# A triangle update followed by a gated pair layer: how the turn from rows to channels is ordered

## The chip, the cores and the metric

The kernel runs on one core of one Trainium2 chip. A core has a matrix engine (PE, with its weight loads shown apart as PEld), a vector engine (DVE), an activation engine (ACT), a general engine (POOL) and a synchronisation engine (SP) that here only issues DMA transfers. Each engine runs its own queue of instructions in order and waits for the others through semaphores. The metric is the device time of one execution in microseconds; lower is better. Three runs of the kernel before took 3364.26, 3364.52 and 3364.75 us; the median is 3364.52 us.

## The reference, cut to what matters

The input x is a square of 384 x 384 positions with 128 channels, all float32. Two layers follow each other.

```python
# layer 0
z_n = layernorm(z)                                   # over the 128 channels
a = (z_n @ Wa + ba) * sigmoid(z_n @ Wga + bga)
b = (z_n @ Wb + bb) * sigmoid(z_n @ Wgb + bgb)
x = einsum('bijd,bjkd->bikd', a, b)                  # for each channel d: a 384x384 matrix product
x = layernorm(x)                                     # over the channels
y = z + (x @ Wo + bo) * sigmoid(z_n @ Wgo + bgo)
# layer 1, on pair = y
left  = pair @ W_left + b_left + pair @ W_eq + b_eq
right = sum over k of (pair @ W_right + b_right)     # one vector for each row i
out   = (left * right * sigmoid(pair @ W_gate + b_gate)) @ W_out + b_out
return layernorm(out + pair)
```

The norm over channels in the middle and the product over j are at odds: a and b are made position by position with all channels, and the product wants one channel with all positions. So a and b are turned from one layout to the other by way of the chip's main memory.

## The kernel before, in words

The kernel has three phases, each written out as a fixed order of instructions; nothing is reordered by a scheduler. Waits between engines and the reuse of tile buffers are derived from the program by the tile layer: an instruction waits for the last users of the memory that it overwrites and for the writers of what it reads, in on-chip memory and in main memory alike.

**Phase 1, by rows.** The square is cut into NT = 72 tiles of 128 rows by CX = 16 columns; tile n covers row block n // 24 and columns 16 (n mod 24) onwards. A tile is worked in TS = 4 steps of CT = 4 columns, so there are 288 steps. For each step s the function `step` (line 199) puts the work in this order. PE: projections pga, pa, pgb (`proj`, line 215), the transposes of the next step's normalised input (`turn`, line 168), pb, and the output gate's projection pgo (line 252). ACT: the sigmoid of pga, the sigmoid of the step before's output gate into the tile gt (`gate`, line 178), two normalisations of a later step, the sigmoid of pgb, the copy of the turned input from PSUM to the tile zT (`turned_out`, line 171), two more normalisations. DVE: statistics of a later tile, the gated at (line 234), the gated bt (line 247), and pgo plus its bias into gs (line 254). The results leave for four arrays in main memory: A[d, j, i] and B[d, j, k] by channel, G (the output gates) and Z (x plus the last bias) by position. POOL issues A (line 238), G (line 185) and Z (line 160), each 1 MB for a tile. B is gathered over CG = 64 columns, four tiles, in a tile bt of 32 KB in each partition; SP issues it in four pieces of BR = 32 rows and 1 MB (`store_b`, line 266), one piece at the end of each following tile, so that the pieces of a group leave during the next group. The last group has no next group: after the last step all pieces that remain go out at once (line 264). Rows of B in such a piece are 64 columns, 256 bytes, long.

On-chip buffers of phase 1 that matter here: four xt tiles, two of each at, gt, bt and zb, three zT, three gs, six PSUM banks for projections (pk) and two for the transposes.

**Phase 2, by channels.** For each channel d, `fetch` (line 433) loads A[d] and B[d] whole, 0.59 MB each, through SP; `product` (line 447) does three products of 128 rows by 384, each of NB = 3 matmuls that add up over the three thirds q of j. Channel 0 is kept as x0 (ACT, line 456). For the others DVE subtracts x0 (line 459), ACT squares (line 464), POOL and DVE keep the running sums s1 and s2 (lines 466 and 445), and SP stores the result to X (line 467). LAST = 8 channels of loads fit on chip; loads run AHEAD = 6 channels in front, and the last eight channels are done block of rows by block of rows so that `deviation` (line 394), the norm's factors, can start early.

**Phase 3, by rows again.** It reads X, G and Z (`load`, line 379), applies the norm and layer 0's output, and does layer 1. The change leaves its instructions as they are; some of its tiles lie elsewhere.

SP's queue thus carries, in order: the loads of xt with the B pieces between them, then the loads of A and B by channel with the stores of X between them, then phase 3's loads. An SP transfer also waits for the one eight places before it.

Of the kernel before, what the change touches and what calls it, by code (L numbers as in the profile page):

```python
# [19 lines left out]
def kernel(ctx: ExitStack, tc: tile.TileContext, ins, out: bass.AP):  # L20
# [25 lines left out]
    A = dram.tile([P, N, N], FP, tag="A", name="A")  # L46
# [31 lines left out]
    wT, bcol = {}, {}  # L78
# [3 lines left out]
    def over(t, n):  # L82
        return t[:, None, :].to_broadcast([P, n, C])
# [4 lines left out]

    CG, CX, CT, BR = 64, 16, 4, 32
    TS = CX // CT
    NT = NB * (N // CX)
    with tc.tile_pool(name="wprep", bufs=6) as wp, tc.tile_pool(name="p1x", bufs=4) as px, tc.tile_pool(name="p1s", bufs=3) as ps, tc.tile_pool(
        name="p1o", bufs=2
    ) as po, tc.tile_pool(name="p1t", bufs=2, space=PSUM) as ppt, tc.tile_pool(
        name="p1p", bufs=6, space=PSUM
    ) as ppp:
        tiles, turned, bts, gated, b_out_of = {}, {}, {}, {}, []
# [5 lines left out]
        def fetch(n):  # L105
            for _ in fetch_parts(n, 1):
                pass
# [46 lines left out]
        def residual(n):  # L154
            if n >= NT:
                return
            r0, c0 = place(n)
            zb = po.tile([P, CX, C], FP, tag="zb", name=f"zb_{n}")
            nc.gpsimd.tensor_tensor(zb, tiles[n]["x"], over(b_out, CX), ALU.add)  # L159
            nc.gpsimd.dma_start(out=Z[r0 : r0 + P, c0 : c0 + CX, :], in_=zb)  # L160

# [9 lines left out]
        def turned_out(s):  # L171
            if s // TS >= NT:
                return
            zT = ps.tile([P, CT, P], FP, tag="zT", name=f"zT_{s}")
            nc.scalar.copy(zT, turned[s])  # L175
            turned[s] = zT

        def gate(s):
            n, t = divmod(s, TS)
            gs = gated.pop(s)  # L180
            gt = tiles[n]["gt"]
            nc.scalar.activation(gt[:, t * CT : (t + 1) * CT, :], gs, AF.Sigmoid)
            if t == TS - 1:
                r0, c0 = place(n)
                nc.gpsimd.dma_start(out=G[r0 : r0 + P, c0 : c0 + CX, :], in_=gt)
                tiles.pop(n - 1, None)


        CATCH_UP = 3 * TS
# [9 lines left out]
        def step(s):  # L199
            n, t = divmod(s, TS)  # L200
            r0, c0 = place(n)
            if t == 0:
                fetch(n + 3)
                if s >= CATCH_UP:
                    norm_factors(n + 1)
                tiles[n]["at"] = po.tile([P, CX, P], FP, tag="at", name=f"at_{n}")
                tiles[n]["gt"] = po.tile([P, CX, C], FP, tag="gt", name=f"gt_{n}")
                if c0 % CG == 0:
                    bts[n // (CG // CX)] = po.tile([P, P, CG], FP, tag="bt", name=f"bt_{n}")
            at, bt = tiles[n]["at"], bts[n // (CG // CX)]  # L210
            k0 = c0 % CG + t * CT
            zT = turned.pop(s)
            ahead = (n + 1, t - 1) if t else (n, TS - 1)

            def proj(k):
                pk = ppp.tile([P, CT, P], FP, tag="pk", name=f"p{k}_{s}")
                nc.tensor.matmul(pk, lhsT=wT[k], rhs=zT, start=True, stop=True)  # L217
                return pk

            def sigmoid(k, pg):  # L220
                sg = ps.tile([P, CT, P], FP, tag="sg", name=f"sg{k}_{s}")
                nc.scalar.activation(sg, pg, AF.Sigmoid, bias=bcol["g" + k])  # L222
                return sg

            statistics(columns_ahead(s), columns_ahead(s + 1))
            for factors in FIRST_FACTORS.get(s, ()):
                norm_factors(*factors)
            pga, pa = proj("ga"), proj("a")
            sga = sigmoid("a", pga)
            if s:  # L230
                gate(s - 1)
            if s >= CATCH_UP:
                normalise(*ahead, range(CT // 2))
            nc.vector.scalar_tensor_tensor(  # L234
                at[:, t * CT : (t + 1) * CT, :], pa, bcol["a"], sga, ALU.add, ALU.mult
            )
            if t == TS - 1:
                nc.gpsimd.dma_start(out=A[:, c0 : c0 + CX, r0 : r0 + P], in_=at)  # L238
            pgb = proj("gb")
            sgb = sigmoid("b", pgb)  # L240
            turn(s + 1)
            turned_out(s + 1)
            if s == 0:
                normalise(0, 2)
            normalise(*ahead, range(CT // 2 if s >= CATCH_UP else 0, CT))
            pb = proj("b")
            nc.vector.scalar_tensor_tensor(  # L247
                bt[:, :, k0 : k0 + CT].rearrange("d r c -> d c r"), pb, bcol["b"], sgb, ALU.add, ALU.mult
            )
            pgo = ppp.tile([P, CT, C], FP, tag="pk", name=f"pgo_{s}")  # L250
            for c in range(CT):
                nc.tensor.matmul(pgo[:, c, :], lhsT=zT[:, c, :], rhs=wT["go"], start=True, stop=True)  # L252
            gs = ps.tile([P, CT, C], FP, tag="gs", name=f"gs_{s}")
            nc.vector.tensor_tensor(gs, pgo, over(gate_bias, CT), ALU.add)
            gated[s] = gs
            if s < CATCH_UP:
                if s in FIRST_RESIDUALS:
                    residual(FIRST_RESIDUALS[s])
            elif t == 1:
                residual(n + 1)  # L260
            if k0 + CT == CG:
                b_out_of.extend((bt, r0, c0 + CX - CG, k) for k in range(0, P, BR))
            if t == TS - 1:
                store_b(len(b_out_of) if n == NT - 1 else 1)

        def store_b(pieces):
            for bt, r0, k0, r in b_out_of[:pieces]:
                nc.sync.dma_start(out=B[:, r0 + r : r0 + r + BR, k0 : k0 + CG], in_=bt[:, r : r + BR, :])
            del b_out_of[:pieces]

        def weight(k, q):
            w = wp.tile([P, P], FP, tag="w", name="w_" + k)
# [85 lines left out]
        for s in range(NT * TS):  # L358
            step(s)
            if s >= CATCH_UP:  # L360
                next(later, None)
        gate(NT * TS - 1)

# [2 lines left out]

    sums = ctx.enter_context(tc.tile_pool(name="sums", bufs=1, reuse_waits="tile"))
    x0, s1, s2, rs0 = (sums.tile([P, NB, N], FP, tag=k, name=k) for k in ("x0", "s1", "s2", "rs0"))
    nc.gpsimd.memset(s1, 0.0)
    nc.gpsimd.memset(s2, 0.0)
    LAST, AHEAD, R = 8, 6, 4
    pl = ctx.enter_context(tc.tile_pool(name="p3l", bufs=3, reuse_waits="tile"))
    group = {}

    def load(u):
# [14 lines left out]
    def deviation(ib, bank):  # L394

        def work(k):
            return sums.tile([P, N], FP, tag="w" + k, name=f"{k}_{ib}")
# [25 lines left out]
        for _ in range(n):  # L423
            next(g, None)

    with tc.tile_pool(name="p2", bufs=LAST, reuse_waits="tile") as p2, tc.tile_pool(
        name="p2s", bufs=12, reuse_waits="tile"
    ) as p2s, tc.tile_pool(name="p2p", bufs=5, space=PSUM, reuse_waits="tile") as pp2, tc.tile_pool(
        name="p2q", bufs=2, space=PSUM, reuse_waits="tile"
    ) as pq2, tc.tile_pool(name="p2t", bufs=1, space=PSUM, reuse_waits="tile") as pt2:  # L430
        factors, squares = {}, []

        def fetch(d):
            if d >= C:
                return
            ad = p2.tile([P, NB, N], FP, tag="ad", name=f"ad_{d}")
            bd = p2.tile([P, NB, N], FP, tag="bd", name=f"bd_{d}")
            nc.sync.dma_start(out=ad, in_=A[d].rearrange("(q p) i -> p q i", p=P))
            nc.sync.dma_start(out=bd, in_=B[d].rearrange("(q p) k -> p q k", p=P))
            factors[d] = ad, bd  # L440
# [6 lines left out]
        def product(d, ib):  # L447
            ad, bd = factors[d]
            pm = pp2.tile([P, N], FP, tag="pm", name=f"pm_{d}_{ib}")
            for q in range(NB):  # L450
                nc.tensor.matmul(  # L451
                    pm, lhsT=ad[:, q, ib * P : (ib + 1) * P], rhs=bd[:, q, :],
                    start=(q == 0), stop=(q == NB - 1),
                )
            if d == 0:
                nc.scalar.copy(by_third(x0[:, ib, :]), pm.rearrange("i (p q) -> i q p", q=NB))
                return
# [8 lines left out]
            nc.gpsimd.tensor_tensor(s1[:, ib, :], s1[:, ib, :], xd, ALU.add)  # L466
            nc.sync.dma_start(out=X[ib][d], in_=xd)

        for d in range(AHEAD):
            fetch(d)  # L470
        for d in range(C - LAST):
            fetch(d + AHEAD)
            for ib in range(NB):
                product(d, ib)
        for d in range(C - LAST + AHEAD, C):
            fetch(d)
        behind = None
        for ib in range(NB):
            if ib == NB - 1:
# [189 lines left out]
```

## Time and profile before

| what | value |
|---|---|
| median of three runs | 3364.52 us |
| the profiled execution's own time | 3363.57 us |
| its span | 3361.8 us |
| PE busy | 3288.6 us, 98% of the span |
| PEld busy | 2191.5 us, 65% |
| DVE busy | 2665.4 us, 79% |
| ACT busy | 2310.0 us, 69% |
| POOL busy | 2093.2 us, 62% |
| DMA | 910.52 MB, mean 271 GB/s |
| phase 1 | from the start to about 1392 us |
| phase 2 | first product at 1423.13 us, last at about 2170 us |

The profile comes from one execution; its span differs from the median of the runs by less than 0.1%. PE's busy time is an average over three phases with different limits, so a wait is read in its own stage. Matmuls are pipelined, and their ends are modelled. In the groups, the columns are the line of the program, engine, operation, what is written and read, the count, then busy time and mean of one in ns, and last the idle time just before, with what ended it. In the chain of waits each line is a start, a length and what the time was spent on. In the tables by stage the pairs are busy time and count of PE, PEld, DVE, ACT and POOL, followed by the clock that PE was granted, the mean busy share of the DMA engines and GB/s.

### The profile page before, as it was taken

What the parts mean: (1) busy time and instruction counts of PE and PEld (TensorE: products, weight loads), DVE (VectorE), ACT (ScalarE), POOL (GpSimd) and SP (SyncE); (2) the same over time, 40 slices, a digit from 0 to 9 for tenths busy, and PEclk for the clock granted to TensorE, in tenths of its full rate; (3) what the DMA queues carried; (4) which work ended last, traced back from release to release, by engine and by line L of the source; (5) the groups of instructions that cost most, each with busy time, mean ns of one, the idle gap of its engine ahead of it and who ended that gap; (6) DMA issues with size and microseconds to landing.
All of it is one profiled execution on the core that took longest, in us unless ns stands there. A gap on an engine that the chain in (4) does not pass through costs nothing.

```text
span 3361.8 us, 53349 instructions
## 1 busy us (share of the span) xinstructions
PE 3288.6 (98%) x15581; PEld 2191.5 (65%) x15581; DVE 2665.4 (79%) x8599; ACT 2310.0 (69%) x5488; POOL 2093.2 (62%) x1574
## 2 busy tenths in 40 slices
PE   8999999999999999699999999999999999999997
PEld 5555555555555555355555555578888888888885
DVE  8877777777777777345555555799999999999998
ACT  7787777877877877422222222378888888888887
POOL 7555555555555555145555555458888888888887
PEclk9999999999999999799999999999999999999998
DMA  6888888888888898799999999767777777777774
GB/s 225 263 262 274 280 277 288 274 284 280 273 263 266 275 282 277 221 340 304 307 304 305 307 306 305 260 228 263 263 264 263 264 263 264 263 263 263 263 264 141
DMA packets 675330, 910.52 MB, mean 271 GB/s; under 512 B 319328, under 2 KB 616288, under 8 KB 647520
## 3 DMA queue, kind: packets, MB, share of 16 engines
q1 hardware_dynamic: 634000, 680.28, 63.0%
q0 software_dynamic: 40320, 226.51, 19.2%
q8 instruction: 126, 2.06, 0.2%
q14 instruction: 164, 1.34, 0.1%
q10 hardware_dynamic: 720, 0.33, 0.0%
HBM read 454.04 MB, written 452.98 MB: 270 GB/s over the span
## 4 chain that ended last, share of the span: by engine, by line
PE 92%; DVE 5%; DMA 1%; POOL 1%; SPq 0%; ACT 0%; issue 0%; POOLq 0%; ACTq 0%; DVEq 0%
PE pm L451 22%; PE pgo L252 8%; PE pga L217 7%; PE pa L217 7%; PE pb L217 7%; PE pgb L217 7%; PE py L546 7%; PE pf L536 7%; PE pleft L587 7%; PE pg L589 6%; PE ptr L168 4%; PE ptr L510 3%; DVE py L552 1%; DVE st L557 1%; DVE h L524 1%; DVE res L537 1%
## 5 line engine op out<-in xcount | busy, mean ns | idle before, releaser
L451 PE MATMUL pm<-bd,ad 128*128 128x384 f32 x2304 | 745.8, 487 | 31.6 <-DMA bd<-B 31.6
L451 PEld LDWEIGHTS pm<-bd,ad 128*128 128x128 f32 x2304 | 438.8, 191 | 337.7 <-issue 33.9
L466 POOL TENSOR_TENSOR s<-s,xd 128x384 f32<-128x384 f32 x381 | 380.2, 998 | 395.6 <-DVE xd L459 395.4
L464 ACT ACTIVATE sq<-xd 128x384 f32<-128x384 f32 x381 | 188.5, 495 | 544.9 <-DVE xd L459 544.9
L247 DVE SCALAR_TENSOR_TENSOR bt<-pb,c_L_conv_bb,sgb 128x512 f32<-128x512 f32 x288 | 321.6, 1117 | 242.6 <-ACT zT L175 232.8
L459 DVE TENSOR_TENSOR xd<-pm,x 128x384 f32<-128x384 f32 x381 | 212.2, 557 | 376.3 <-POOL s L466 321.0
L149 ACT ACTIVATE zn<-xt,off,rstd 128x128 f32<-128x128 f32 x1152 | 503.3, 489 | 2.9 <-POOL off L140 2.8
L579 ACT ACTIVATE res<-res,off,rs 128x128 f32<-128x128 f32 x1152 | 482.3, 485 | 20.4 <-POOL off L573 18.6
L552 DVE SCALAR_TENSOR_TENSOR py<-py,rs,gr 128x128 f32<-128x128 f32 x1152 | 436.6, 379 | 1.6 <-PE py L546 1.0
L238 POOL DMA_DIRECT2D A<-at x72 | 85.5, 1188 | 544.1 <-DVE at L234 544.1
L252 PEld LDWEIGHTS pgo<-wT_go,zT 128*128 128x128 f32 x2304 | 302.5, 192 | 137.7 <-issue 72.0
L222 ACT ACTIVATE sga<-pga,c_L_conv_bga 128x512 f32<-128x512 f32 x288 | 197.9, 687 | 274.8 <-PE pga L217 274.8
L557 DVE BATCH_NORM_STATS2 st<-res 128x6 f32<-128x128 f32 x1152 | 364.4, 317 | 0.3
L619 POOL TENSOR_TENSOR res<-res,r_L_conv_ln_bias 128x1536 f32<-128x1536 f32 x94 | 324.8, 3455 | 7.4
L159 POOL TENSOR_TENSOR zb<-xt,r_L_conv_b_out 128x2048 f32<-128x2048 f32 x72 | 327.1, 4544 | 1.8
L536 PE MATMUL pf<-w_o,h 128*128 128x128 f32 x2304 | 321.2, 276 | 6.1 <-ACT w_o L518 5.3
L618 POOL TENSOR_TENSOR res<-res,r_L_conv_ln_scale 128x1536 f32<-128x1536 f32 x94 | 325.5, 3463 | 0.1
L546 PE MATMUL py<-w_o,xr 128*128 128x128 f32 x2304 | 320.8, 275 | 0.9 <-DVE xd L459 0.9
L594 ACT ACTIVATE sg<-pg,c_L_conv_b_gate 128x384 f32<-128x384 f32 x384 | 223.2, 581 | 141.9 <-PE pg L589 90.5
L587 PE MATMUL pleft<-pairT,m_L_conv_W_left 128*128 128x384 f32 x768 | 313.0, 489 | 2.9 <-ACT pairT L512 2.8
L589 PE MATMUL pg<-pairT,m_L_conv_W_gate 128*128 128x384 f32 x768 | 311.1, 487 | 0.0
L130 DVE BATCH_NORM_STATS2 st<-xt 128x6 f32<-128x128 f32 x1152 | 306.1, 266 | 3.6 <-DMA xt<-in_x_dram 3.6
(131 smaller groups left out, 6818.9 us busy)
## 6 DMA issues: line engine op xcount, KB each, us to landing
A<-at POOLq DMA_DIRECT2D x72, 1024.0 KB, 8.3
Z<-zb POOLq DMA_DIRECT2D x72, 1024.0 KB, 8.2
G<-gt POOLq DMA_DIRECT2D x72, 1024.0 KB, 8.7
B<-bt SPq DMA_DIRECT2D x72, 1024.0 KB, 16.9
ad<-A SPq DMA_DIRECT2D x128, 576.0 KB, 7.0
bd<-B SPq DMA_DIRECT2D x128, 576.0 KB, 8.0
xr<-X SPq DMA_DIRECT2D x96, 768.0 KB, 6.0
gr<-G SPq DMA_DIRECT2D x96, 768.0 KB, 7.6
```

Of the source, the lines that this page charges most:

```text
L149: nc.scalar.activation(g["zn"][:, c, :], g["x"][:, c, :], AF.Identity, bias=g["off"][:, c : c + 1], scale=g["rstd"][:, c : c + 1],)
L217: nc.tensor.matmul(pk, lhsT=wT[k], rhs=zT, start=True, stop=True)
L252: nc.tensor.matmul(pgo[:, c, :], lhsT=zT[:, c, :], rhs=wT["go"], start=True, stop=True)
L451: nc.tensor.matmul(pm, lhsT=ad[:, q, ib * P : (ib + 1) * P], rhs=bd[:, q, :], start=(q == 0), stop=(q == NB - 1),)
L466: nc.gpsimd.tensor_tensor(s1[:, ib, :], s1[:, ib, :], xd, ALU.add)
L536: nc.tensor.matmul(pf[:, q, :], lhsT=h[:, q * P : (q + 1) * P], rhs=w_o, start=True, stop=True)
L546: nc.tensor.matmul(py[:, q, :], lhsT=g["x"][:, i, q * P : (q + 1) * P], rhs=w_o0, start=True, stop=True)
L552: nc.vector.scalar_tensor_tensor(py[:, q, :], py[:, q, :], rs0[:, q, u : u + 1], g["g"][:, i, q, :], ALU.mult, ALU.mult)
L557: nc.vector.bn_stats(b["st"][:, k, q, :], b["res"][:, k, q, :])
L579: nc.scalar.activation(g["res"][:, i, q, :], g["res"][:, i, q, :], AF.Identity, bias=g["off"][:, i, q : q + 1], scale=g["rs"][:, i, q : q ...
L587: nc.tensor.matmul(pleft, lhsT=w_left, rhs=pairT, start=True, stop=True)
L589: nc.tensor.matmul(pg[:, 0:N], lhsT=w_gate, rhs=pairT, start=True, stop=True)
```

## The change

- **Gate projections of the last group.** For the last TG = 4 tiles, steps S2 = 272 to 287, pgo and gs are taken out of `step` into a function `gate_project` and done after all steps, one behind the other, with the sigmoids following one place later. Since zT is then read long after its step, `turned_out` writes it into the tile xt for those steps.
- **The last group's b.** It is not stored by rows. Its tile is allocated so that it stays on chip through most of phase 2 (`pb_held`), and `store_held` stores it by HELD = 16 channels: 16 partitions, 128 rows of 256 bytes, 0.52 MB. The first goes between the loads of the first four channels, the second after those of channel 5, six more inside the loop over channels, at d = 14, 30, 46, 62, 78 and 94.
- **First products by thirds.** Channels 0 to 3 are loaded in two parts: thirds 0 and 1 of j first, which the last row block does not touch, and third 2 after the first held store. The first two thirds of five products (EARLY) are multiplied before the loop, and `product` adds the last third.
- **Memory.** zb uses the memory that later holds x0, s1, s2 and rs0 (`acc`). The two bt tiles come from two pools of one. A[d] and B[d] share one tile ab, and phase 2's tiles are allocated from the other end of on-chip memory. The pools of `deviation` and of phase 3's loads open after the held tile is freed.

The diff without empty lines and without the renamed pools of unchanged tiles:

```diff
+    S2 = (NT - TG) * TS
+    acc = acc.tile([P, 4, NB, N], FP, tag="acc", name="acc")
+    pb_held = held.enter_context(tc.tile_pool(name="p1bh", bufs=1))
...
-            zb = po.tile([P, CX, C], FP, tag="zb", name=f"zb_{n}")
+            zb = acc.rearrange("p a q n -> p (a q n)")[:, (n % 2) * CX * C : (n % 2 + 1) * CX * C]
...
-            zT = ps.tile([P, CT, P], FP, tag="zT", name=f"zT_{s}")
+            if s < S2:
+                zT = ps.tile([P, CT, P], FP, tag="zT", name=f"zT_{s}")
+            else:
+                n, t = divmod(s, TS)
+                zT = tiles[n]["x"][:, t * CT : (t + 1) * CT, :]
...
+        def gate_project(s):
+            n, t = divmod(s, TS)
+            if t == 0:
+                tiles[n]["gt"] = pgt.tile([P, CX, C], FP, tag="gt", name=f"gt_{n}")
+            zT = turned[s]
+            pgo = ppp.tile([P, CT, C], FP, tag="pk", name=f"pgo_{s}")
+            for c in range(CT):
+                nc.tensor.matmul(pgo[:, c, :], lhsT=zT[:, c, :], rhs=wT["go"], start=True, stop=True)
+            gs = ps.tile([P, CT, C], FP, tag="gs", name=f"gs_{s}")
+            nc.vector.tensor_tensor(gs, pgo, over(gate_bias, CT), ALU.add)
+            gated[s] = gs
...
-            if s:
+            if 0 < s <= S2:
                 gate(s - 1)
...
+            if s < S2:
+                gate_project(s)
...
-            if k0 + CT == CG:
+            if k0 + CT == CG and n < NT - 1:
                 b_out_of.extend((bt, r0, c0 + CX - CG, k) for k in range(0, P, BR))
...
+        for s in range(S2, NT * TS):
+            gate_project(s)
+            if s > S2:
+                gate(s - 1)
         gate(NT * TS - 1)
+        b_held = bts[NT // TG - 1]
...
+        def store_held(d):
+            if d < C:
+                nc.sync.dma_start(out=B[d : d + HELD, N - P :, N - CG :], in_=b_held[d : d + HELD])
...
-        for d in range(AHEAD):
+        EARLY = ((0, 0), (0, 1), (0, 2), (1, 0), (1, 1))
+        for d in range(4):
+            fetch(d, 0, NB - 1)
+        store_held(0)
+        for d in range(4):
+            fetch(d, NB - 1)
+        for d in range(4, AHEAD):
             fetch(d)
+        store_held(HELD)
+        for d, ib in EARLY:
+            multiply(d, ib, range(NB - 1))
         for d in range(C - LAST):
             fetch(d + AHEAD)
+            if (d + 2) % HELD == 0:
+                store_held(d + 2 + HELD)
             for ib in range(NB):
                 product(d, ib)
...
+        held.close()
+        work_of = ctx.enter_context(tc.tile_pool(name="work", bufs=1, reuse_waits="tile"))
```

More of the change, by code (lines that the diff above doesn't have):

```diff
@@ L91 @@
     CG, CX, CT, BR = 64, 16, 4, 32
-    TS = CX // CT
+    TS, TG = CX // CT, CG // CX
     NT = NB * (N // CX)
-    with tc.tile_pool(name="wprep", bufs=6) as wp, tc.tile_pool(name="p1x", bufs=4) as px, tc.tile_pool(name="p1s", bufs=3) as ps, tc.tile_pool(
-        name="p1o", bufs=2
-    ) as po, tc.tile_pool(name="p1t", bufs=2, space=PSUM) as ppt, tc.tile_pool(
+    S2 = (NT - TG) * TS
+    acc = ctx.enter_context(tc.tile_pool(name="acc", bufs=1, reuse_waits="tile"))
+    acc = acc.tile([P, 4, NB, N], FP, tag="acc", name="acc")
+    held = ExitStack()
+    pb_held = held.enter_context(tc.tile_pool(name="p1bh", bufs=1))
+    with tc.tile_pool(name="wprep", bufs=6) as wp, tc.tile_pool(name="p1s", bufs=3) as ps, tc.tile_pool(
+        name="p1g", bufs=2
+    ) as pgt, tc.tile_pool(name="p1x", bufs=4) as px, tc.tile_pool(name="p1a", bufs=2) as pa_, tc.tile_pool(
+        name="p1b", bufs=1, side="right"
+    ) as pb_, tc.tile_pool(name="p1t", bufs=2, space=PSUM) as ppt, tc.tile_pool(
         name="p1p", bufs=6, space=PSUM
@@ L157, in residual @@
             r0, c0 = place(n)
-            zb = po.tile([P, CX, C], FP, tag="zb", name=f"zb_{n}")
+            zb = acc.rearrange("p a q n -> p (a q n)")[:, (n % 2) * CX * C : (n % 2 + 1) * CX * C]
+            zb = zb.rearrange("p (x c) -> p x c", x=CX)
             nc.gpsimd.tensor_tensor(zb, tiles[n]["x"], over(b_out, CX), ALU.add)
@@ L205, in step @@
                     norm_factors(n + 1)
-                tiles[n]["at"] = po.tile([P, CX, P], FP, tag="at", name=f"at_{n}")
-                tiles[n]["gt"] = po.tile([P, CX, C], FP, tag="gt", name=f"gt_{n}")
+                tiles[n]["at"] = pa_.tile([P, CX, P], FP, tag="at", name=f"at_{n}")
                 if c0 % CG == 0:
-                    bts[n // (CG // CX)] = po.tile([P, P, CG], FP, tag="bt", name=f"bt_{n}")
-            at, bt = tiles[n]["at"], bts[n // (CG // CX)]
+                    bts[n // TG] = (pb_ if (NT - 1 - n) // TG % 2 else pb_held).tile(
+                        [P, P, CG], FP, tag="bt", name=f"bt_{n}"
+                    )
+            at, bt = tiles[n]["at"], bts[n // TG]
             k0 = c0 % CG + t * CT
-            zT = turned.pop(s)
+            zT = turned[s]
             ahead = (n + 1, t - 1) if t else (n, TS - 1)
@@ L249, in step @@
             )
[L250 to L255, printed above, removed]
+            if s < S2:
+                gate_project(s)
             if s < CATCH_UP:
@@ L260, in step @@
                 residual(n + 1)
-            if k0 + CT == CG:
+            if k0 + CT == CG and n < NT - 1:
                 b_out_of.extend((bt, r0, c0 + CX - CG, k) for k in range(0, P, BR))
[L263 to L267, printed above, removed]
+            if t == TS - 1 and b_out_of:
+                bt, r0, k0, r = b_out_of.pop(0)
                 nc.sync.dma_start(out=B[:, r0 + r : r0 + r + BR, k0 : k0 + CG], in_=bt[:, r : r + BR, :])
-            del b_out_of[:pieces]
         def weight(k, q):
@@ L361 @@
                 next(later, None)
+        for s in range(S2, NT * TS):
+            gate_project(s)
+            if s > S2:
+                gate(s - 1)
         gate(NT * TS - 1)
+        b_held = bts[NT // TG - 1]
     def by_third(t):
         return t.rearrange("i (q p) -> i q p", q=NB)
-    sums = ctx.enter_context(tc.tile_pool(name="sums", bufs=1, reuse_waits="tile"))
-    x0, s1, s2, rs0 = (sums.tile([P, NB, N], FP, tag=k, name=k) for k in ("x0", "s1", "s2", "rs0"))
+    x0, s1, s2, rs0 = (acc[:, k] for k in range(4))
     nc.gpsimd.memset(s1, 0.0)
     nc.gpsimd.memset(s2, 0.0)
-    LAST, AHEAD, R = 8, 6, 4
-    pl = ctx.enter_context(tc.tile_pool(name="p3l", bufs=3, reuse_waits="tile"))
+    LAST, AHEAD, R, HELD = 8, 6, 4, 16
     group = {}
@@ L396, in work @@
         def work(k):
-            return sums.tile([P, N], FP, tag="w" + k, name=f"{k}_{ib}")
+            return work_of.tile([P, N], FP, tag="w" + k, name=f"{k}_{ib}")
         v, t, r, sg, sd = (work(k) for k in ("v", "t", "r", "sg", "sd"))
@@ L424, in advance @@
             next(g, None)
-    with tc.tile_pool(name="p2", bufs=LAST, reuse_waits="tile") as p2, tc.tile_pool(
-        name="p2s", bufs=12, reuse_waits="tile"
+    with tc.tile_pool(name="p2", bufs=1, side="right", reuse_waits="tile") as p2, tc.tile_pool(
+        name="p2s", bufs=12, side="right", reuse_waits="tile"
     ) as p2s, tc.tile_pool(name="p2p", bufs=5, space=PSUM, reuse_waits="tile") as pp2, tc.tile_pool(
@@ L430, with pair_of, fetch @@
     ) as pq2, tc.tile_pool(name="p2t", bufs=1, space=PSUM, reuse_waits="tile") as pt2:
-        factors, squares = {}, []
-        def fetch(d):
+        factors, products, squares = {}, {}, []
+        def pair_of(d):
+            return p2.tile([P, 2, NB, N], FP, tag=f"ab{d % LAST}", name=f"ab_{d}")
+        for d in reversed(range(LAST)):
+            factors[d] = pair_of(d)
+        def fetch(d, q0=0, q1=NB):
             if d >= C:
                 return
[L436 to L440, printed above, removed]
+            if d not in factors:
+                factors[d] = pair_of(d)
+            for k, of in enumerate((A, B)):
+                nc.sync.dma_start(
+                    out=factors[d][:, k, q0:q1], in_=of[d, q0 * P : q1 * P].rearrange("(q p) i -> p q i", p=P)
+                )
+        def store_held(d):
+            if d < C:
+                nc.sync.dma_start(out=B[d : d + HELD, N - P :, N - CG :], in_=b_held[d : d + HELD])
         def add_squares():
@@ L445, in add_squares, with multiply, product @@
                 nc.vector.tensor_tensor(s2[:, ib, :], sq, s2[:, ib, :], ALU.add)
[L447 to L450, printed above, removed]
+        def multiply(d, ib, qs):
+            ab = factors[d]
+            if 0 in qs:
+                products[d, ib] = pp2.tile([P, N], FP, tag="pm", name=f"pm_{d}_{ib}")
+            for q in qs:
                 nc.tensor.matmul(
-                    pm, lhsT=ad[:, q, ib * P : (ib + 1) * P], rhs=bd[:, q, :],
+                    products[d, ib], lhsT=ab[:, 0, q, ib * P : (ib + 1) * P], rhs=ab[:, 1, q, :],
                     start=(q == 0), stop=(q == NB - 1),
                 )
+        def product(d, ib):
+            multiply(d, ib, range(NB) if (d, ib) not in products else range(NB - 1, NB))
+            pm = products.pop((d, ib))
             if d == 0:
@@ L476 @@
             fetch(d)
+        held.close()
+        work_of = ctx.enter_context(tc.tile_pool(name="work", bufs=1, reuse_waits="tile"))
+        pl = ctx.enter_context(tc.tile_pool(name="p3l", bufs=3, reuse_waits="tile"))
         behind = None
```

## The prediction

> **What bounds the kernel now.** I read the table of slices first: PE is at eight or nine tenths nearly everywhere, with one dip to 6 in slice 17, near 1400 us. Then the costliest groups (busy us, mean ns | idle before and its releaser):
>
> ```profile
> L451 PE MATMUL pm<-bd,ad 128*128 128x384 f32 x2304 | 745.8, 487 | 31.6 <-DMA bd<-B 31.6
> ```
>
> All 2304 product matmuls together wait once, 31.6 us, for a load of B. The chain of waits around that place (start us, us, what):
>
> ```profile
> 1390.78 1.10 DVE bt L247
> 1392.30 7.31 SPq L268
> 1399.66 7.50 SPq L268
> 1407.20 11.36 DMA B<-bt
> 1418.65 4.35 DMA bd<-B
> 1423.13 77.08 PE pm L451 x231
> ```
>
> The last b is written at 1391.9; its four 1 MB stores leave until 1418.65, and only then is B loaded. The stages there (busy us of PE, PEld, DVE, ACT, POOL; then granted clock, DMA share, GB/s):
>
> ```profile
> 1380.00:1390.00 10.00, 10.00 (x42) 5.85 (x41) 5.03 (x7) 4.83 (x9) 0.00 (x0) 1.00 0.00 2
> ...
> 1405.00:1410.00 5.00, 0.00 (x0) 0.00 (x0) 0.00 (x0) 0.00 (x0) 0.00 (x0) 0.50 0.85 216
> ...
> 1423.00:1427.00 4.00, 3.87 (x6) 2.19 (x7) 0.00 (x0) 0.00 (x0) 0.00 (x0) 0.50 1.03 362
> ```
>
> DMA does nothing in the 10 us before the turn; then 256-byte pieces move at 216 GB/s while PE stands; then PE restarts at half clock. So this turn is bound by data, everything around it by PE. Last, the timeline of the step before the last one, for what a step is bound by:
>
> ```profile
> 1382.31 1.02 PE L217 MATMUL pga<-zT,wT_ga 128*128 128x512 f32 x2
> ...
> 1384.02 1.02 PE L217 MATMUL pgb<-zT,wT_gb 128*128 128x512 f32 x2
> ...
> 1384.88 0.60 PE L168 MATMUL ptr<-ident,zn 128*128 128x128 f32 x4
> ...
> 1385.14 0.69 ACT L222 ACTIVATE sgb<-pgb,c_L_conv_bgb 128x512 f32<-128x512 f32 x1 [0.57 <-PE pgb L217]
> ...
> 1385.73 0.58 ACT L175 COPY zT<-ptr 128x512 f32<-128x512 f32 x1
> ...
> 1386.18 1.05 PE L252 MATMUL pgo<-wT_go,zT 128*128 128x128 f32 x8
> ...
> 1387.07 1.02 PE L217 MATMUL pga<-zT,wT_ga 128*128 128x512 f32 x2
> ```
>
> Step to step is 4.765 us, filled by PE; pgo holds 0.89 of it. The copy of the next zT ends at 1386.31, while PE is still in pgo.
>
> [...] clock 0.50 until about 1427.7. [...] No store of 16 partitions is in this trace. [...]
>
> **The change part by part.** S is the end of the last step's pb on PE.
>
> 1. *Gate projections of the last 16 steps move behind all steps.* Each step loses 0.89 of PE work: 4.765 − 0.886 = 3.88. But PE was the cover for ACT. The order there is sgb, then the zT copy, and the next pga needs zT. From pga, the copy ends at 1386.31 − 1382.31 = 4.00; a PE matmul started 0.06 after its ACT releaser elsewhere (2178.94 to 2179.00). So a step takes 4.06. ACT's two pairs of zn and DVE's statistics, at and bt (1.8 + 0.75 + 1.1 = 3.65) fit in that. Fifteen intervals by 0.705 = 10.6 us: the last pga falls from 1387.07 to 1376.5. The last step is then pga, pa, pgb, pb, 4 × 0.86 = 3.44: S = 1379.9. Its bt ends at S + 1.4 = 1381.3. The sixteen projections take 16 × 0.886 = 14.2: PE busy until 1394.1. They need nothing that is late: zT now stays in the x tiles. PE's idle inside the steps is 16 × 0.18 = 2.9 us, a real cost.
>
> 2. *What is queued behind the gates.* The gt tile has two buffers. Tile 70's first sigmoid waits until tile 68's G store has landed, and DVE's gs has three buffers, so DVE stalls behind ACT, and the second and third early products wait for the last two gs (PSUM banks). With gs 0.67 and gt 0.62: G of tile 68 is issued at S + 5.5, of tile 69 at S + 9.1. If a G store lands after L us, the last but one gs ends at about S + 8.9 + L, and the second early product could start at S + 15.5. So PE waits about L − 6.3. G landed after 8.4 us at the busy end of phase 1, and 7.8 in a lighter stretch. I take L = 8, a stall of 1.75 us; L = 6 gives 0, L = 12 gives 5.7.
>
> 3. *Loads by thirds, first two thirds early.* In the built program the first load waits for the last store of the group before (issued at 1337.5, 10 us of issue; landed by about 1355) and A of tiles up to 63. Four pairs of two thirds, 3.1 MB, move in the idle stretch; at 216 GB/s they need 15 us: there by 1370, 24 us before use. The five early products are 10 matmuls by 0.643 = 6.4 us of PE work, so the last thirds are wanted at 1394.1 + 1.75 + 6.4 = 1402.3.
>
> 4. *The held b.* SP issues the first 0.52 MB store at 1381.3. The bytes take 2.4 us at 216 GB/s[...]; the first bd load, 0.59 MB, landed in 4.35 us of which 1.6 are bytes at 376 GB/s, so 2.8 us are fixed. That makes 5 to 8 us: landed by 1389. A of tile 71 (issued 1379.5, 6.3 to 8 us) lands by 1387.5. Behind them: the loads of d = 0's last thirds, 4.4 (the first bd load) to 8 us (median): 1393 to 1397. Slack 5 us or more; cost nothing, with the projections and early products as cover. The later loads have more time: d = 4 is wanted at about 1419. Traffic until then: A 1.05, G 4.2, held 0.5, thirds 1.6, d = 4 1.2 MB, 8.5 MB in 37 us or 230 GB/s; 373 were seen.
>
> 5. *Six more held stores inside the product loop* (d = 14 to 94), two before. On SP each stands behind a load and ahead of three X stores. PE never waited for data in phase 2 after its start, and a load is issued six products (35 us) ahead and lands in 8: 27 us of lead against 5 to 8 us for a store. Cost nothing; without that cover, 6 × 5 to 8.
>
> 6. *Memory moved* (acc for zb and sums, b on the right, pair tiles, work tiles later). It changes what the first phase 3 tiles wait for, but those in the built program are stores and loads long landed or the same ones as before. Nothing; from −2 us, if a wait at the start of phase 3 goes, to +2, if one comes. The number of PE, DVE, ACT and POOL operations is the same.
>
> **Sum.** The first product starts at 1394.1 in place of 1423.13: −29.0. No cold start: the steady end of the eighth product counted back by 8 × 1.935 us puts a warm start at 1425.4 against 1423.1: −2.3. Gate stall: +1.75. Together −29.6. Checked by PE's idle: −31.6 − 2.3 + 2.9 + 1.75 = −29.3. The profiled execution took 3363.57 (span 3361.8), the median of the runs is 3364.52, 0.03% apart, so the sum applies to both: 3364.5 − 29.5 = 3335.0 us.
>
> **The rivals.**
> - *The steps don't get shorter*, because ACT or DVE paces them at 4.765. For it: ACT is 8.06 of 10 us busy. Against: 0.62 of each step is the moved gt. Then S is 1390.5, products at 1404.7: −18.4 − 2.3 + 1.75 = −19: 3345.5.
> - *The turn is still dry*: G at L = 12, or thirds late by some us in the pile of G, A and held stores after 1381. For it: 11 MB are issued within 20 us. Against: the slack of 5 us. Costs 4 to 9 us more: 3339 to 3344.
> - *Slower: held stores choke the loads.* If a store of 16 partitions ran on one engine at 216 / 16 = 13.5 GB/s, it would take 39 us, more than the 27 us of lead. The first would delay the turn to about the old time; six more stall PE by some 12 us each: about 3430. It is slower than before from about 32 us per store (six by 5 us eat the gain). [...]
> - *It does nothing*: if the first loads had to wait for all of B. The built program's waits exclude it; 3364.
>
> **Chances.** The forecast, 3331 to 3339: 0.70. Still dry, 3339 to 3344: 0.14. Steps not shorter, 3344 to 3349: 0.08. Slower: 0.04. Nothing: 0.02. Below 3331: 0.02. The range 3331 to 3344 holds about 0.84. A measurement of this kernel can tell about 0.2%, 6.7 us, from no change: faster 0.94, same 0.02, slower 0.04.
>
> **What would show it.** pga to pga 4.06 us in the last 16 steps, with ACT's zT as releaser; sixteen pgo back to back for 14.2 us; early pm matmuls from about 1394 at clock 1.00, with a wait of 1 to 3 us on DVE gs; a first held store landing in 5 to 8 us; no PE wait on DMA in the product loop; phase 3 as long as before. Wrong would be: a wait of pm on ab loads above 1 us, steps of 4.7, or held stores above 27 us.

## The result, and the profile after

The kernel after takes 3340.09 us (median of six runs, 3339.17 to 3343.24), against 3363.81 us for the kernel before beside it (3363.24 to 3364.75). The ratio is 0.993, 95% interval 0.992 to 0.9939. The forecast was 3335.0 us, range 3331 to 3344. So most of the forecast gain came, and 5.1 us of it did not. The measured time lies in the upper part of the range, 3339 to 3344, which the prediction kept for a rival; the forecast proper was 3331 to 3339. The profiled execution took 3343.24 us (span 3341.5); it is the slowest of the six, so a sum against this profile has 9.2 us to explain: 3343.24 less the forecast's 3363.57 − 29.5 = 3334.1.

The same three views as before. Costliest groups (busy us, mean ns | idle before and its releaser): the products' one wait fell from 31.6 to 5.8 us, and it is no longer a load that ends it.

```profile
L488 PE MATMUL pm<-ab 128*128 128x384 f32 x2304 | 746.6, 487 | 5.8 <-DVE gs L213 5.8
```

The chain of waits around the turn (start us, us, what):

```profile
1381.37 3.58 PE pgo L211 x32
...
1386.70 12.75 DMA G<-gt
...
1399.53 0.64 ACT gt L198
...
1400.19 0.04 DVE gs L213
...
1401.99 0.69 DVE gs L213
...
1402.73 37.40 PE pm L488 x106
```

Where four B stores stood before, there is now one store of G, 12.75 us from issue to landing. Tile 70's gate gt needs the buffer that this store empties, the next gs needs that gate, and PE needs the PSUM bank that gs reads. The store's own line, among the issues of DMA from 1380 to 1400 (KB each, us from issue to landing):

```profile
B<-bt SPq DMA_DIRECT2D x1, 512.0 KB, 14.3
```

This B<-bt is the first held store. The timeline of PE, SP and POOL in the same place (start us, us, engine, line, and in brackets the idle before and its releaser):

```profile
1373.58 1.12 PE L246 MATMUL pga<-xt,wT_ga 128*128 128x512 f32 x2
...
1377.67 1.13 PE L246 MATMUL pga<-xt,wT_ga 128*128 128x512 f32 x2
...
1381.21 14.45 PE L211 MATMUL pgo<-wT_go,xt 128*128 128x128 f32 x128
...
1382.62 0.33 SPq L476 DMA_DIRECT2D B<-bt  x1
...
1386.70 0.56 POOL L201 DMA_DIRECT2D G<-gt  x1 [4.73 <-ACT gt L198]
...
1395.50 1.46 PE L488 MATMUL pm<-ab 128*128 128x384 f32 x4
1396.96 0.33 SPq L470 DMA_DIRECT2D ab<-B  x1
...
1402.73 1.65 PE L488 MATMUL pm<-ab 128*128 128x384 f32 x2 [5.77 <-DVE gs L213]
```

Steps are 4.09 us apart, the sixteen projections follow without a gap, and the first early product starts at 1395.50. The held store is issued at 1382.62; it landed 14.3 us later, and only then does SP issue the first of the last thirds of B (1396.96). The stages (busy us and count of PE, PEld, DVE, ACT, POOL; then granted clock, DMA share, GB/s):

```profile
1383.00:1387.00 4.00, 4.00 (x38) 4.00 (x37) 3.04 (x6) 2.85 (x5) 0.30 (x1) 1.00 0.93 248
1387.00:1391.00 4.00, 4.00 (x38) 4.00 (x37) 3.19 (x5) 2.19 (x4) 0.81 (x2) 1.00 0.60 77
1391.00:1395.00 4.00, 4.00 (x38) 4.00 (x38) 0.79 (x2) 0.00 (x0) 0.00 (x0) 1.00 0.72 134
1395.00:1399.00 4.00, 1.95 (x10) 1.07 (x9) 0.00 (x0) 0.00 (x0) 0.00 (x0) 1.00 0.97 381
...
1403.00:1407.00 4.00, 4.00 (x7) 2.19 (x8) 0.69 (x1) 2.19 (x4) 0.93 (x2) 0.50 1.02 353
```

The second and third lines matter. From 1387 to 1391 DMA moves 77 GB/s, though a megabyte of G is waiting; before the change the 256-byte pieces of B went at 216. And after the wait PE runs at half clock once more in this execution (last line), as in the kernel before.

The trace's own list of DMA pieces shows what moves. Counted by the microsecond that begins at the time on the left (number of pieces that start in it, and in brackets the mean ns of one; the columns name the transfer and the bytes of a piece):

```
            A, 4096 B      held b, 256 B     G, 8192 B
1385        70 (228)        -                 -
1387        -               304 (32)          -
1390        -               294 (33)          -
1392        -               139 (53)          8 (386)
1395        -               22 (85)           35 (350)
```

The held store starts when A of tile 71 is through, at 1386.2, so 3.6 of its 14.3 us pass before its first piece. Then its pieces go at 300 per us, and no piece of G, issued at 1386.70, moves before 1392; A of tile 71, with nothing ahead of it, was issued at 1380.81 and moved from 1382.5. The times of the pieces of one us add up to 9.6 us, as if 9.6 of 16 DMA engines were at work (the stage's DMA share is 0.60). Two things were open: whether the held store is to blame or the count of gt buffers, and if it is the store, whether the cause is its 16 neighbouring partitions.

### The profile page after: what moved, and what is told of

It reads as the page before. It is cut to its first block, busy times and chain, and to the rows that moved or that the text cites. A ratio compares the mean times of both kernels' runs of the same rounds, so it can differ in the third digit from the quotient of the medians.

```text
span 3341.5 us, 53397 instructions
## 1 busy us (share of the span) xinstructions
PE 3293.7 (99%) x15581; PEld 2191.3 (66%) x15581; DVE 2666.1 (80%) x8599; ACT 2311.3 (69%) x5488; POOL 2091.9 (63%) x1574
## 4 chain that ended last, share of the span: by engine, by line
PE 96%; DVE 2%; POOL 1%; DMA 1%; ACT 0%; issue 0%; POOLq 0%; ACTq 0%; SPq 0%; DVEq 0%
PE pm L488 22%; PE pga L246 8%; PE pa L246 7%; PE pgb L246 7%; PE pb L246 7%; PE py L602 7%; PE pf L592 7%; PE pgo L211 7%; PE pleft L643 7%; PE pg L645 7%; PE ptr L180 4%; PE ptr L566 4%; DMA G<-gt 0%; DVE py L608 0%; PE pg L656 0%
## 5 line engine op out<-in xcount | busy, mean ns | idle before, releaser
L488 PE MATMUL pm<-ab 128*128 128x384 f32 x2304 | 746.6, 487 | 5.8 <-DVE gs L213 5.8
L488 PEld LDWEIGHTS pm<-ab 128*128 128x128 f32 x2304 | 438.9, 191 | 312.4 <-DVE gs L213 6.7
L507 POOL TENSOR_TENSOR acc<-acc,xd 128x384 f32<-128x384 f32 x381 | 380.1, 998 | 362.4 <-DVE xd L500 362.2
L500 DVE TENSOR_TENSOR xd<-pm,acc 128x384 f32<-128x384 f32 x381 | 212.2, 557 | 343.3 <-POOL acc L507 321.3
L608 DVE SCALAR_TENSOR_TENSOR py<-py,acc,gr 128x128 f32<-128x128 f32 x1152 | 433.7, 377 | 2.2 <-PE py L602 1.6
L211 PEld LDWEIGHTS pgo<-wT_go,zT 128*128 128x128 f32 x2176 | 285.7, 192 | 130.0 <-issue 66.5
L171 POOL TENSOR_TENSOR acc<-xt,r_L_conv_b_out 128x2048 f32<-128x2048 f32 x72 | 327.4, 4548 | 1.8
```

What stands on the lines that cost most here:

```text
L488: nc.tensor.matmul(products[d, ib], lhsT=ab[:, 0, q, ib * P : (ib + 1) * P], rhs=ab[:, 1, q, :], start=(q == 0), stop=(q == NB - 1),)
L608: nc.vector.scalar_tensor_tensor(py[:, q, :], py[:, q, :], rs0[:, q, u : u + 1], g["g"][:, i, q, :], ALU.mult, ALU.mult)
```

## The experiments

All ran beside the kernel before (3363.40 to 3364.25 us in the three sets), so a difference below 1 us between kernels of different sets is not read. The two kernels of experiment 2 have two runs each, the others four to seven. A summary first; "wait" is PE's idle before the product matmuls, and "half clock" the stretch at the turn, both in the profiled execution:

| kernel | median us (lowest to highest) | wait of pm, and for what | half clock |
|---|---|---|---|
| after | 3340.09 (3339.17–3343.24) | 5.8, gs | 1401.9–1408.7 |
| gates in the x tiles | 3340.95 (3338.92–3342.21) | 4.4, last thirds of B | 1407.8–1414.6 |
| first held store over 128 partitions | 3334.67 (3334.40–3334.94) | 0.3, gs | none |
| first held store left out | 3335.30 (3335.24–3335.37) | 0.9, gs | none |
| held stores over spread partitions | 3335.66 (3335.44–3337.36) | 1.4, gs | none |
| ... and the turn first | 3332.88 (3331.79–3333.88) | 1.7, gs | none |
| spread, gates in the x tiles | 3333.43 (3333.13–3333.64) | 0.0 | none |
| spread, turn first, gates in x | 3330.66 (3330.16–3330.98) | 0.0 | none |
| gates inside the steps | 3343.67 (3343.16–3344.16) | 10.4, thirds of B | 1402.1–1412.3 |
| whole loads | 3345.92 (3345.83–3346.85) | 8.9, B | 1398.2–1408.5 |
| last b by rows | 3353.83 (3353.45–3355.68) | 17.4, B and gs | 1407.7–1424.7 |

**1. Gates in the x tiles.** The output gates of the last four tiles are written over the x tiles, whose last reader is the projection; no sigmoid then waits for an earlier G store.

```diff
-            gt = tiles[n]["gt"]
+            gt = tiles[n]["gt"] if s < S2 else tiles[n]["x"]
...
-            if t == 0:
+            if t == 0 and s < S2:
```

> The gates of the last four tiles are written into the x tiles, which hold zT until then, so no gate waits for a G store to land; everything else is as in the changed kernel. Theory (the gate buffers cost 5.8 us of waiting and about 2.9 us of half clock after it): PE has no wait on DVE gs, goes on at clock 1.00 until about 1402, then waits 1 to 2 us for the last thirds, since the first held store is unchanged; 6 to 7 us less in the profiled execution, about 3334 to 3336 us. Rival (the wait only moves: the last thirds of B are what PE ends up waiting for anyway): PE restarts at 1402 to 1404 as before and the time stays at 3339 to 3341 us.

Measured: 3340.95 us, ratio 0.993 (0.9917 to 0.9942), no different from after: the rival's range, not the theory's. The wait for gs is gone and another has come. Groups and timeline (the ten early matmuls are recorded as two each, hence x20):

```profile
L488 PE MATMUL pm<-ab 128*128 128x384 f32 x2304 | 746.9, 488 | 4.4 <-DMA ab<-B 4.4
```

```profile
1395.27 6.62 PE L488 MATMUL pm<-ab 128*128 128x384 f32 x20
...
1403.43 2.17 PE L488 MATMUL pm<-ab 128*128 128x384 f32 x6 [1.54 <-DMA ab<-B]
...
1408.49 11.69 PE L488 MATMUL pm<-ab 128*128 128x384 f32 x26 [2.88 <-DMA ab<-B]
```

The early products now run at once, but use up the cover: the last thirds, issued only when the held store has landed, come late: with four G stores under way beside them, B's took 10.5 us from issue to landing (median of three, issued from 1380 to 1402), where the first two of after took 6.3. PE drops to half clock just the same, though neither wait is as long as the one of after. So the gt buffers are where the delay showed, not its source.

**2. The same bytes from 128 partitions, and no first store.** The first held store is replaced by one of the same size and piece length, 16 rows of all 128 channels; or it is left out. The added line puts the b of the group before in its place, so part of the result is missing in both.

```diff
+        nc.sync.dma_start(out=B[0:HELD, N - P :, N - CG :], in_=bts[NT // TG - 2][0:HELD])
...
-        store_held(0)
+        nc.sync.dma_start(out=B[:, N - P : N - P + 16, N - CG :], in_=b_held[:, 0:16])
```

The second kernel has the added line and no store in the place of `store_held(0)`.

> The first held store is replaced by one of the same bytes and the same 256-byte pieces that takes 16 rows of all 128 channels; channels 0 to 15 of the last row block get the b of the group before (a store of 16 channels in the idle stretch near 1360), so the result leaves that out. Theory (16 partitions are what makes the held store slow): its 2048 pieces pass in 2.5 to 3.5 us in place of 6.7, the G store of tile 68 lands 4 us sooner (about 8 to 9 us after its issue), PE waits 2 us or less for gs, and the time is 4 to 6 us below the changed kernel. Rival (the pieces are slow because they meet the A and G stores): the pieces still take 6 us or more, G lands after 12 us, same time.

> No first held store at all; channels 0 to 15 of the last row block get the b of the group before in the idle stretch near 1360, so the result leaves that out. Theory: the G store of tile 68 lands 6 to 8 us after its issue, so by my formula (wait = landing less 6.3) PE waits 0 to 2 us for gs, no half clock, and the last thirds are there by about 1395: 7 to 8 us below the changed kernel, 3331 to 3334 us. Rival (G lands late for its own sake or because of the loads): G still lands after 11 us or more, PE waits 4 us or more, the time falls by less than 3 us.

Measured: 3334.67 us, ratio 0.9912 (0.9894 to 0.9931), and 3335.30 us, 0.9914 (0.9896 to 0.9932). The stages and the timeline of the first:

```profile
1383.00:1387.00 4.00, 4.00 (x39) 4.00 (x38) 2.92 (x6) 2.78 (x5) 0.56 (x1) 1.00 0.92 248
1387.00:1391.00 4.00, 4.00 (x39) 4.00 (x38) 3.19 (x5) 1.63 (x3) 0.55 (x1) 1.00 0.99 337
```

```profile
1396.37 23.83 PE L488 MATMUL pm<-ab 128*128 128x384 f32 x72 [0.23 <-DVE gs L213]
```

337 GB/s stand where 77 stood. The pieces went at 840 per us, 16 ns each, and were through in 2.8 us; G of tile 68 landed in 7.2 us; PE waited 0.2 us and kept its clock. With no store at all the time is the same within 0.6 us. So the first held store costs about 5 us as it stands and next to nothing when as many bytes leave from all partitions. The kernel with no store came out 1.3 us above what was expected of it: PE still waited 0.9 us for gs, and its projections start at 1381.75, 0.5 later than after's.

**3. Sixteen partitions, but spread.** The channels are worked in the order 0, 8, 16 and so on, and a held store takes every eighth partition. Number, size and piece length of the stores are those of after.

```diff
+        SKIP = C // HELD
+        def channel(d):
+            return d % HELD * SKIP + d // HELD
...
-                    out=factors[d][:, k, q0:q1], in_=of[d, q0 * P : q1 * P].rearrange("(q p) i -> p q i", p=P)
+                    out=factors[d][:, k, q0:q1], in_=of[channel(d), q0 * P : q1 * P].rearrange("(q p) i -> p q i", p=P)
...
-                nc.sync.dma_start(out=B[d : d + HELD, N - P :, N - CG :], in_=b_held[d : d + HELD])
+                nc.sync.dma_start(out=B[d // HELD :: SKIP, N - P :, N - CG :], in_=b_held[d // HELD :: SKIP])
...
-            nc.sync.dma_start(out=X[ib][d], in_=xd)
+            nc.sync.dma_start(out=X[ib][channel(d)], in_=xd)
```

> The products take the channels in the order 0, 8, 16, ... 120, 1, 9, ..., and a held store takes 16 partitions that lie 8 apart in place of 16 neighbours; bytes, pieces and counts are as in the changed kernel. Theory (the first held store is slow [...]): its pieces pass at about twice the 300 in a us that 16 neighbours gave, in 3 to 4 us; the G store of tile 68 lands 9 to 10 us after its issue, PE waits 3 us or less for gs and keeps its full clock: 3334 to 3337 us, 3 to 6 us below the changed kernel. Rival (what counts is that only 16 partitions are read, wherever they lie): pieces still at 300 in a us, the time stays at 3339 to 3341 us.

Measured: 3335.66 us, ratio 0.9919 (0.9904 to 0.9933), 4.4 us below after. The issues of DMA from 1381 to 1392 (KB each, us from issue to landing), and the timeline:

```profile
G<-gt POOLq DMA_DIRECT2D x2, 1024.0 KB, 8.2
A<-at POOLq DMA_DIRECT2D x1, 1024.0 KB, 6.7
B<-bt SPq DMA_DIRECT2D x1, 512.0 KB, 8.9
```

```profile
1398.08 2.37 PE L493 MATMUL pm<-ab 128*128 128x384 f32 x6 [1.40 <-DVE gs L213]
```

The held store lands in 8.9 us, in place of 14.3 in after and 12.0 to 13.9 in the other three kernels that keep it, at 600 to 660 pieces per us and about 20 ns each; PE waits 1.4 us and keeps its clock. So most of the slowness came with the sixteen neighbouring channels, not with the count of sixteen or the 256-byte pieces. The edit spreads the places in B along with the partitions, and so did experiment 2; no run tells the two sides apart. The rates while the store moved were 77 GB/s from sixteen neighbours, about 160 (630 pieces of 256 bytes) from every eighth partition and 215 (840 pieces) from all 128. That the partitions are the cause, and not the places in B, was the author's estimate; it was not shown.

**4. What each part of the change is worth.** One part undone at a time: the gate projections back inside the steps; no thirds and no early products; the last b stored by rows as before.

```diff
-    S2 = (NT - TG) * TS
+    S2 = NT * TS
```

```diff
-        EARLY = ((0, 0), (0, 1), (0, 2), (1, 0), (1, 1))
-        for d in range(4):
-            fetch(d, 0, NB - 1)
         store_held(0)
-        for d in range(4):
-            fetch(d, NB - 1)
-        for d in range(4, AHEAD):
+        for d in range(AHEAD):
             fetch(d)
...
-        for d, ib in EARLY:
-            multiply(d, ib, range(NB - 1))
```

```diff
-            if k0 + CT == CG and n < NT - 1:
+            if k0 + CT == CG:
...
-        store_held(0)
+        for bt, r0, k0, r in b_out_of:
+            nc.sync.dma_start(out=B[:, r0 + r : r0 + r + BR, k0 : k0 + CG], in_=bt[:, r : r + BR, :])
...
-        store_held(HELD)
...
-            if (d + 2) % HELD == 0:
-                store_held(d + 2 + HELD)
```

> The gate projections stay in their steps, as before the change; the held b, the thirds and the early products stay as changed. Theory (moving the projections is worth what its 9 us of earlier b are worth at the turn): the last b is written at 1392, the first held store lands about 9 to 12 us later, the early products run from about 1392 to 1398, PE then stands until the last thirds land at 1406 to 1410 and starts cold, 2 to 3 us: 3341 to 3346 us, 1 to 6 us above the changed kernel. Rival (the projections cover the whole turn): 9 us or more above the changed kernel, 3349 or later.

> No thirds and no early products: after the first held store the channels are loaded whole, as before the change; the rest is as changed. Theory: in the changed kernel most early products ran only after the wait for gs, so the thirds hide little; without them the first product starts at 1403 to 1406, cold: 3341 to 3345 us, 1 to 5 us above. Rival (the early loads are worth their full 6.4 us of products and more): 3346 us or later.

> The last group's b leaves by rows as before the change, four stores of 1 MB after the last step, and no held stores; the late gate projections, the loads by thirds and the early products stay. Theory (the held store is what lets the turn end early, 0.5 MB in place of 4): the four stores are done at 1405 to 1415, the last thirds land 5 us later, PE stands and starts cold: 3346 to 3355 us, 6 to 15 us above the changed kernel. Rival (the slow 16-partition store eats what its fewer bytes save): 3340 to 3344 us.

Measured: 3343.67 us (0.994, 0.9924 to 0.9955), 3345.92 us (0.9949, 0.9932 to 0.9966) and 3353.83 us (0.9972, 0.9961 to 0.9983): 3.6, 5.8 and 13.7 us above after. In this order, each from its own timeline:

```profile
1409.24 11.12 PE L488 MATMUL pm<-ab 128*128 128x384 f32 x29 [10.36 <-DMA ab<-B]
```

```profile
1404.63 15.68 PE L488 MATMUL pm<-ab 128*128 128x384 f32 x42 [8.89 <-DMA ab<-B]
```

```profile
1382.24 28.34 SPq L515 DMA_DIRECT2D B<-bt  x4
...
1419.67 0.98 PE L488 MATMUL pm<-ab 128*128 128x384 f32 x1 [15.76 <-DMA ab<-B]
```

In all three PE stands for B until about 1405 to 1420. The held store is the largest part: without it the four stores by rows take 28 us on SP (the SPq line) ahead of the last thirds. The thirds are worth more than the theory gave them (3341 to 3345), 0.1 us short of the rival's 3346: nearly all of their 6.4 us. The moved projections are worth least: without them the last step ends later but the early products start 3.2 us earlier (1392.27), and what changes is mainly how long PE then waits. In the two profiled executions the spans are even the same (3341.6 and 3341.5); only the medians differ.

**5. The versions that the findings point to.** First the spread kernel, with the transposes of the next step ahead of pgb on PE and the copy of zT ahead of the sigmoid sgb on ACT in the last sixteen steps, since ACT's copy was what the next pga waited for.

```diff
+            if s >= S2:
+                turn(s + 1)
             pgb = proj("gb")
+            if s >= S2:
+                turned_out(s + 1)
             sgb = sigmoid("b", pgb)
-            turn(s + 1)
-            turned_out(s + 1)
+            if s < S2:
+                turn(s + 1)
+                turned_out(s + 1)
```

> As the kernel with the spread channels, and in the last 16 steps the transposes of the next step come before pgb on PE and the zT copy before sgb on ACT. Theory (a step of 4.09 us is the chain pgb, sgb, zT, pga): a step falls to 3.88 to 3.92 us, the last b is written 2.5 to 3 us earlier, and the time is 2 to 3.5 us below the kernel with spread channels alone: 3331 to 3335 us. Rival (the turn is bound by its DMA traffic, so an earlier end of the steps is eaten by a longer wait there): less than 1 us below it.

Measured: 3332.88 us, ratio 0.9909 (0.9894 to 0.9924), 2.8 us below the spread kernel. Steps are 3.87 us apart (pga at 1366.35, 1370.22, 1374.09), and the projections start at 1377.53 in place of 1380.93. Fifteen steps by 0.22 us are 3.3; the wait for gs, 0.35 us longer, takes part of it back.

That wait is the one that experiment 1 took away in vain. With a quick held store it was tried again, with and without the turn:

> As the run before with spread partitions and the turn first (3332.9 us, wait for gs 1.75 us), but the output gates of the last four tiles go into the x tiles, so that no sigmoid waits for an earlier G store. Theory (with a quick held store only the gt buffers are left of the wait): pm starts where pgo ends, about 1392, the last thirds are issued from about 1388 and land by 1397, before their use at 1398.5; 1.5 to 2 us less, 3331 us (3330 to 3332). Rival (the four G stores now leave within 11 us and crowd the last thirds, as they did with the slow held store): the wait moves to ab<-B, 1 to 3 us, and the time stays at 3332 to 3335.

> As the run with spread partitions alone (3335.7 us, wait for gs 1.4 us), with the output gates of the last four tiles in the x tiles. Theory (only the gt buffers are left): pm starts at about 1395.5 without a wait and the time falls by about 1.4 us to 3334.3 (3333.5 to 3335). Rival (G crowds the last thirds): a wait on ab<-B of 1 us or more and 3335 to 3338.

Measured: 3330.66 us, ratio 0.99 (0.9885 to 0.9915), and 3333.43 us, 0.9908 (0.9892 to 0.9925): 2.2 us below the kernel without it in both cases (3.1 if each is taken against the kernel before of its own set). Groups, stages and chain of the first:

```profile
L498 PE MATMUL pm<-ab 128*128 128x384 f32 x2304 | 743.4, 486 | 0.0
```

```profile
1390.00:1394.00 4.00, 4.00 (x29) 3.34 (x28) 2.68 (x4) 2.91 (x5) 0.53 (x1) 1.00 1.01 372
1394.00:1398.00 4.00, 4.00 (x14) 2.41 (x13) 0.00 (x0) 0.00 (x0) 2.60 (x3) 1.00 1.03 372
```

```profile
1378.19 14.29 PE pgo L211 x128
1392.48 47.73 PE pm L498 x148
```

No product waits for anything, and DMA moves 372 GB/s under it. The same edit was worth nothing on top of the slow store and 2.2 us on top of the quick one. This version is 9.4 us faster than after.

## Why the prediction was right or wrong

The number came out inside the range, but not by the forecast's own mechanism. The range reached to 3344 because it took in the rival *The turn is still dry*, and that rival's wait for G is what happened. That the time stayed within the range was in part luck: the rival put the wait down to 11 MB of traffic in 20 us, and the runs show one slow store of half a megabyte in its place.

**The step of the last sixteen: right.** Predicted 4.06 us, from sgb and the zT copy; measured 4.09, with ACT's copy as the releaser of the weight load of every pga, and experiment 5 shows it by moving the copy. The sixteen projections took 14.29 us against 14.2. The first early product started at 1395.50, not 1394.1: 0.6 us of this is that the last group begins later (pga of step 272 at 1316.20 against 1315.58 before), 0.5 the fifteen intervals, and 0.1 each the last step and the projections. Term: +1.4.

**The gate wait: right formula, wrong L.** The prediction's chain, G's landing, gt, gs, PSUM bank, early product, is the chain of the profile. It gave a wait of L − 6.3, which is 6.4 us at the measured L of 12.75; the wait was 5.77. L was taken from the end of phase 1 of the kernel before, where no held store runs beside G. Term: +4.0, the measured wait less the 1.75 us that were forecast.

**No cold start: wrong in the profiled execution.** The prediction took off 2.3 us because PE would not stop for long; that its 1.75 us would keep the clock was the author's estimate. With a wait of 5.8 us PE did stop for long: the trace shows 0.50 from about 1401.9 to 1408.7, of which PE was working 6.0 us, so it lost 3.0. The prediction's rival names no such loss beside its longer waits. Nor was so long a wait needed: the clock fell 4.9 us after PE had stopped in after (1396.96 to about 1401.9), but 2.2 us after it in the kernel before (1391.56 to 1393.73), and again 2.2 us after it in experiment 1 (1405.60 to 1407.81), in a wait of only 2.88 us. Waits of up to 1.75 us, the longest in the spread kernel with the turn first, kept the clock. Term: +3.0.

The three terms are 8.4 us: 3334.1 + 8.4 = 3342.5, against 3343.24 for the profiled execution. The rest is phase 3: from the transposes pr just ahead of it to the end of the span there are 1193.7 us in place of 1192.9 (they start at 2147.85 and 2168.92).

The other five runs of after lie 2 to 4 us below the profiled one, and the mean granted clock of each run says why in part: it is 0.994 in the profiled execution and 0.996 in the three runs of 3339.2 to 3339.9. A mean of 0.996 leaves room for about 30 us at half clock in a whole run; in every profiled kernel about 26 or more go to the start of phase 3 and to the end, and no stretch at the turn was shorter than 6.8. So, by this estimate, these three passed the turn at full clock, and the +3.0 is not theirs. How long PE waited in them is not shown.

**The held store: the step that failed.** The prediction gave it 5 to 8 us and called it free as it had slack for its own loads. The 5 is worked out from the trace of before, 2.4 us of bytes at 216 GB/s and 2.8 fixed; the 8 was the author's estimate, and no store of 16 partitions had been measured. Measured here: 14.3 us, of which 3.6 waiting behind A of tile 71, and 77 GB/s while it ran alone. Two things followed. The step asked only who waits for the store, not what queues behind it: G of tile 68, issued 0.5 us after its first piece, moved nothing for 5.3 us, where A had taken 1.7 with nothing ahead. And the slack of its own loads was gone too: the first of the last thirds of B landed at 1403.5 (1396.96 and 6.6 us), not at 1393 to 1397, and was wanted by 1402.3. In after nothing waits for it, because PE already stands for gs; with that wait removed, in experiment 1, PE stood 4.4 us for the last thirds. That the slow store is the cause is shown by experiments 2 and 3, where PE's wait falls to 0.2 to 1.4 us. With the store mended as in experiment 3, the kernel takes 3335.66 us, 0.7 from the forecast.

**The other steps.** The six held stores in the product loop cost nothing, as predicted: they land in 9.4 to 10.1 us, longer than the 5 to 8 forecast but inside the 27 us of lead, and PE waits for no load between 1410 and 2140. Moving the memory cost no more than the 0.8 us of phase 3: the longest wait at its start, for pair, is 4.7 us in place of 3.5.

**The rivals.** *The turn is still dry*, 3339 to 3344, with G at L = 12 as its first mechanism, is what happened; it had been given 0.14. *Steps don't get shorter* fell with the 4.09 us. *Held stores choke the loads* fell too, since 13.5 GB/s was far too low against the 77 measured, though nothing in the trace of before had ruled it out; it had seen the right culprit at the wrong size, and in the loop in place of the turn. *It does nothing* fell with the result.

## What to carry to other kernels

Price a transfer by where its pieces lie as well as by its bytes: here half a megabyte in 256-byte pieces went at 77 GB/s from sixteen neighbouring partitions and at 215 from all 128. Then ask what is issued behind it, for the cost of a slow store may land on another queue's store: here G of tile 68 landed in 12.75 us behind the slow one and in 7.2 behind the quick one of experiment 2. A wait of PE is priced with the half clock that may follow it: here 1.75 us did without, 2.88 us had it, and after 5.8 us it added half as much again, 3.0 us. And a second limit is worth trying again once the first is mended: the same edit gave nothing before and 2.2 us after.

## What the runs showed of the hardware that was not expected

- 256-byte pieces of a store went at 840 per us (16 ns each, 215 GB/s) from 128 partitions in experiment 2, 600 to 660 (20 ns, about 160 GB/s) from sixteen partitions eight apart in experiment 3, and 300 (32 ns, 77 GB/s) from sixteen neighbours in after.
- While the store from neighbours ran in after, a store issued on POOL's queue just after its first piece moved no piece for 5.3 us, though the pieces under way accounted for 9.6 of 16 engines (DMA share 0.60). Why the rest stood by is open; the records do not tell which engine carried a piece. Before that the same held store had stood 3.6 us behind a store of POOL's queue.
- The half clock came 2.2 us after PE had stopped, in a wait of 2.88 us (experiment 1) and in the long one of the kernel before; it came 4.9 us after it in after, and not at all in a wait of 1.75 us (the spread kernel with the turn first).
